# Two-layer decoder: expert results scattered to token order, row sends spread over fewer steps, three bias copies placed behind the last expert block

## The chip, the cores and the metric

The kernel runs on one core of one Trainium2 chip. A core has a matrix engine (TensorE, PE in the profile; its weight loads are listed as PEld), three engines for elementwise work (VectorE or DVE, ScalarE or ACT, GpSimd or POOL), a sync engine that only issues transfers (SyncE or SP), and 16 DMA engines that carry all transfers. Each engine runs its own instructions in order; semaphores tie the engines together. The metric is the device time of one execution in microseconds, lower is better.

## The reference, cut to what matters

The program is a pre-norm decoder of two layers over 32 sequences of 100 tokens (3200 tokens of 256 numbers, float32). Each layer has self-attention, cross-attention over 361 context rows, and a mixture of experts. The change touches the end of Layer 0 and the start of Layer 1:

```python
# Layer 0's experts: 8 experts of width 704, the best 2 per token, plus a shared one of width 352
logits = x @ gate_w
top_v, top_i = jax.lax.top_k(logits, 2)
top_p = jax.nn.softmax(top_v, axis=-1)
combine = zeros((T, 8)).at[arange(T)[:, None], top_i].add(top_p)
d = einsum('tei,eih->teh', silu(x @ Wg) * (x @ Wu), Wd)
out = einsum('te,teh->th', combine, d) + silu(x @ Sg) * (x @ Su) @ Sd

# Layer 1's self-attention: causal, no softmax
k, q, v = split(x @ W1 + b1, 3)
attn = where(mask, q @ k^T, 0.0)
out = (attn @ v) @ W2 + b2
```

## The kernel before

The token array x stays in SBUF as 25 tiles of 128 tokens (NF = 25). PE's order is written out by hand; on the other engines the instructions stand in an order that a scheduler finds when the program is built. Waits between engines are derived from the data, and `depend` adds further ones by hand.

**Up to the experts (0 to about 1100 us).** Layer 0's self- and cross-attention. While it runs, SP fills work arrays in device memory (`stage_weights`, L1100 on): all expert weights in one array `w_d`, zeros in `xe_d` (L1115, the rows sorted by expert) and zeros in those parts of `y_d` (L1118, the experts' results in the same order) that belong to blocks that seldom run. Normalized token rows are written into a tile that takes the place of a weight tile, `self.rows` (L455), 256 numbers per row, tile after tile.

**Shared expert and row sends (about 1100 to 1182 us).** PE works through the shared expert in groups of four tiles: `hidden(f)` makes the products w of gate and up (ACT L1197, DVE L1198), and `down(f)` of a group two steps back multiplies by the third matrix and adds into x (DVE L1207). Beside this GpSimd sends each token's row to its two places in `xe_d`: `scatter` (L1158 to L1168) is one indirect DMA of 128 rows (issued at L1160), 50 in all, tile after tile with both choices k = 0 and k = 1 of a tile one after the other. `tick` spreads them: each DVE result of the shared expert is a tick, and after tick t of N_TICKS = 34 (L1209) the same fraction of the 50 sends may have gone. A send waits for the DVE result at whose tick it was placed.

**Expert blocks (1182 to about 1592 us).** 29 blocks run always: 24 of 256 rows and 5 of 128 rows (the fourth, the tenth and so on are such half blocks). For each, `load0` (L1272) lets GpSimd gather the weights of the block's expert (2.2 MB, L1277, three buffers) and SP load the block's rows (L1285, three buffers) two blocks ahead; the load waits for all 50 sends. `turn0` (L1294) transposes the rows on PE while the block before is computed. `block0` (L1326) is six chunks: PE makes gate and up, ACT the activation g, DVE the product h (L1341; for the last chunk of 64 columns a copy u, L1349, and two products, L1354 and L1356), then PE multiplies by the third matrix (L1362, and L1368 for the last chunk), ACT and DVE copy the results to y (L1373, L1374), and SP writes y to `y_d` (L1375). `behind` (L1238) places small work behind chosen blocks, tied to the block's last DVE copy (`self.late`): loads of Layer 1's weights (L1248), and behind the fifth block copies of the slot table and the probabilities (L1241), which Layer 1 needs.

After the 29 blocks every engine reads a count (L1251) and skips the remaining blocks (`tc.If`, L1252) if all rows have been dealt with, as they have in these runs.

**Layer 1's self-attention (about 1595 to 1815 us).** First PE makes values for the following cross-attention (L703, L155 into `v`, ACT L149). `gather0` (L1255) then brings the two expert results of every token: two indirect DMAs per tile on GpSimd by the slot table (issued at L1261, eight buffers), and DVE adds each, times its probability, to x (L1266). Norms follow (DVE L196 to L208, square root on ACT L202), and then the attention itself, sequence by sequence: `proj` (q and k; ACT L973 and L970), `scores` (PE, then DVE L1002 with the mask), `vals` (DVE L983), `values` (PE L1012, ACT L1019), `out` (DVE L260). The gathers and norms of a group of four sequences are spread over the work on an earlier group. Three small DVE operations in `l1_attn` prepare the biases of q and k (L942 twice, L943); the scheduler is free to place them as early as it sees fit.

Layer 1's cross-attention and experts fill the rest.

Of the kernel before, what the change touches and what calls it, by code (L numbers as in the profile page):

```python
# [9 lines left out]
F32 = mybir.dt.float32  # L10
I32 = mybir.dt.int32
# [32 lines left out]

XROW = D + 1 + E1

HALVES = {0: 6, 6: 6, 12: 6, 18: 7}
# [51 lines left out]
class Kernel:  # L99
# [331 lines left out]
    def l0_xattn(self):  # L431
        nc, tc, a = self.nc, self.tc, self.a
        with ExitStack() as st:
# [14 lines left out]
            for h in range(H):  # L448
# [5 lines left out]

            self.rows = self.wts.tile([P, 8192], F32, tag="wA", name="wAn")[:, : NF * D].rearrange(  # L455
                "p (f d) -> p f d", f=NF
            )

# [23 lines left out]
            for t in ks:  # L482
                nc.gpsimd.memset(t[:, :, :, L:], 0.0)
            later = deque()
            ctx, q, q2, e, es = {}, {}, {}, {}, {}
# [435 lines left out]
    def l1_attn(self):  # L921
        nc, tc, a = self.nc, self.tc, self.a
        with ExitStack() as st:
# [17 lines left out]
            for j in range(2):  # L941
                nc.vector.tensor_scalar(bias[:, j, :], bqk[:, 0, :], own[:, j : j + 1], None, ALU.mult)  # L942
            nc.vector.tensor_copy(bias[:, 2, :], bqk[:, 2, :])  # L943
            vs = [cp.tile([T, H, 32], F32, tag=f"v{i}", name=f"v{i}") for i in range(3)]
# [155 lines left out]
    def stage_weights(self):  # L1100


        nc, a = self.nc, self.a
        dram = self.ctx.enter_context(
            self.tc.tile_pool(name="dram0", bufs=1, space=bass.MemoryType.DRAM)
        )
        self.w_d = dram.tile([E0 * P, WROW], F32, tag="w_d", name="w_d")
        self.xe_d = dram.tile([ROWS0, D], F32, tag="xe_d", name="xe_d")
        self.y_d = dram.tile([ROWS0, D], F32, tag="y_d", name="y_d")
        with self.tc.tile_pool(name="zero", bufs=1) as zp:  # L1110
            zero = zp.tile([P, 2048], F32, tag="zero", name="zero")
            nc.gpsimd.memset(zero, 0.0)
            xe = self.xe_d.rearrange("(i p r) d -> i p (r d)", p=P, r=8)
            for i in range(ROWS0 // (8 * P)):
                nc.sync.dma_start(xe[i], zero)  # L1115
            for j in REST0:
                y = self.y_d[rows0(j)[0], :].rearrange("(p r) d -> p (r d)", p=P)
                nc.sync.dma_start(y, zero[:, : y.shape[1]])  # L1118
        for e in range(E0):
            row = self.w_d[e * P : (e + 1) * P, :]  # L1120
            for k in range(NK):
                for j, n in enumerate(("wg0", "wu0")):
                    src = a[n][e][k * P : (k + 1) * P, :]
                    o = k * 2 * I0
                    nc.sync.dma_start(row[:, o + 640 * j : o + 640 * (j + 1)], src[:, :640])
                    nc.sync.dma_start(
                        row[:, o + 1280 + 64 * j : o + 1280 + 64 * (j + 1)], src[:, 640:]
                    )
            o = 2 * NK * I0
            src = a["wd0"][e]  # L1130
            for c in range(5):
                nc.sync.dma_start(row[:, o + c * D : o + (c + 1) * D], src[c * P : (c + 1) * P, :])

            for j in range(2):
                nc.sync.dma_start(row[64 * j : 64 * j + 64, o + 5 * D :], src[640:, :])

    def l0_ffn(self):
# [3 lines left out]
        with ExitStack() as st:  # L1141
# [16 lines left out]
            def scatter(after):  # L1158
                f, k = divmod(len(sent), 2)
                got = nc.gpsimd.indirect_dma_start(  # L1160
                    out=self.xe_d[:, :],
                    out_offset=bass.IndirectOffsetOnAxis(ap=slot[:, f, k : k + 1], axis=0),
                    in_=xn[:, f, :], in_offset=None,
                    bounds_check=ROWS0 - 1, oob_is_err=True,
                )
                tc.declare_no_dep(got.ins, group="xe", reason="other rows")
                tc.add_to_no_dep_group("xe", got.ins)
                self.depend(got, [after.ins], "not faster than the work beside it")  # L1168
                sent.append(got.ins)
# [38 lines left out]

            N_TICKS = NF + 3 * 6 - 9  # L1209
            with tc.manual_schedule(engines={mybir.EngineType.PE}):  # L1210
# [21 lines left out]
            o = 6144 + 1536  # L1232
            slot1 = self.wa1.bitcast(I32)[:, o : o + 2 * NF].rearrange("p (f k) -> p f k", k=2)
            pr21 = self.wa1[:, o + 2 * NF : o + 4 * NF].rearrange("p (k f) -> p k f", k=2)
            self.picked0 = slot1, pr21

            def behind(j):
                if BLOCKS0 - 5 < j < BLOCKS0 - 1:  # L1238
                    self.depend(self.load1(j - BLOCKS0 + 4), [self.late.ins], "behind the block")
                if j == 4:  # L1240
                    for got in (nc.vector.tensor_copy(slot1, slot), nc.vector.tensor_copy(pr21, pr2)):  # L1241
                        self.depend(got, [self.late.ins], "behind the block")

                room = 4 if j > 1 else 0
                while room > 0 and self.loads:
# [3 lines left out]
                    self.depend(got, [self.late.ins], "behind the block")  # L1249
            self.blocks0_run(pool, ORDER0, wid, hs, sent, behind)  # L1250
            n = nc.values_load(self.blocks0[0:1, 0:1], min_val=0, max_val=NBLK)  # L1251
            with tc.If(n > 0):  # L1252
                self.blocks0_run(pool, REST0, wid, hs, [], lambda i: None)

    def gather0(self, pool, f, after=None):  # L1255

        nc = self.nc
        slot, pr2 = self.picked0
        for k in range(2):
            y = pool.tile([P, D], F32, tag="yk", name="yk", bufs=8)  # L1260
            nc.gpsimd.indirect_dma_start(  # L1261
                out=y, out_offset=None, in_=self.y_d[:, :],
                in_offset=bass.IndirectOffsetOnAxis(ap=slot[:, f, k : k + 1], axis=0),
                bounds_check=ROWS0 - 1, oob_is_err=True,
            )
            got = nc.vector.scalar_tensor_tensor(  # L1266
# [6 lines left out]
    def load0(self, pool, j, wid, sent):  # L1273
# [7 lines left out]
        )  # L1281
        xe = pool.tile([P, 2, D], F32, tag="xe", name="xe", bufs=3)
        at, n = rows0(j)
# [10 lines left out]
    def turn0(self, pool, xe):  # L1294
# [8 lines left out]
        self.evac(xT, pt)  # L1303
        return xT

    def blocks0_run(self, pool, js, wid, hs, sent, behind):

        with self.tc.manual_schedule(engines={mybir.EngineType.PE}):
            ready = [self.load0(pool, j, wid, sent) for j in js[:2]]
            w, xe = ready.pop(0)  # L1310
            xT = self.turn0(pool, xe)
            for i, j in enumerate(js):
                got = []
                if i + 2 < len(js):
                    ready.append(self.load0(pool, js[i + 2], wid, sent))

                def turn():
                    if ready:
                        w, xe = ready.pop(0)
                        got.extend((w, self.turn0(pool, xe)))  # L1320

                self.late = self.block0(pool, j, w, xT, hs[i % 2], turn)
                behind(i)
                if got:
                    w, xT = got

    def block0(self, pool, j, w, xT, h, turn):
# [46 lines left out]
        done = nc.vector.tensor_copy(y[:, 0, :], py[0])  # L1374
        nc.sync.dma_start(self.y_d[at, :].rearrange("(s p) d -> p s d", p=P), y)  # L1375
        return done

# [708 lines left out]
```

## Time and profile before

| | us |
|---|---|
| median of 3 runs (lowest to highest) | 2970.16 (2968.84 to 2970.37) |
| profiled execution | 2999.12 |
| its span, first to last instruction | 2997.4 |
| mean granted TensorE clock in it | 0.981 |

The parts of the kernel that the change is about, in the profiled execution:

| what | measured |
|---|---|
| expert block of 256 rows, from weight gather to weight gather | 15.08 to 15.12 us in undisturbed stretches |
| half block | 8.30 us |
| GpSimd row send or gather of 128 rows, one | 0.98 to 1.04 us busy |
| zero fill of `y_d` | 7 transfers, issued between 30.96 and 45.9 us |
| expert results to `y_d` | 29 SP writes, 24 of 256 KB and 5 of 128 KB |
| results back in Layer 1 | 50 GpSimd gathers, 1595.9 to 1720 us |

How to read the lines further down. A line of a timeline has the start (us from the span's start), the length, the engine, the line of the kernel, the operation, output and input tiles, shapes, and how many instructions it stands for; in brackets the engine's idle time just before and what ended it ("issue": nothing that the profile shows). Names of tiles are those of the program: `xe` a block's rows, `w` weights or a product in the same tile, `ps_t` a PSUM bank, `y` a block's result, `yk` a gathered result, `wAn` the normalized rows, `kT` and `qT` keys and queries. A line of windows has the stretch, its length, then busy time and instruction count of PE, PEld, DVE, ACT and POOL, then PE's granted clock as a fraction of full speed, the DMA engines' mean busy share, and GB/s.

### The profile page before, as it was taken

Reading aid. Unit: us, or ns where it says so; the run is one execution under the profiler, and the core shown is the slowest. Engines: PE = TensorE matmul, PEld = TensorE weight load, DVE = VectorE, ACT = ScalarE, POOL = GpSimd, SP = SyncE. Lnnn points to the kernel's source line nnn. Section 1 sums busy time; section 2 is a strip of 40 time slices with the busy share of each in tenths; the row PEclk is TensorE's granted clock in tenths of the full one; section 3 lists DMA queues with packets and bytes.
Section 4 is the critical chain, followed back from the end, with each engine's and each line's share of the span. In section 5 each row is a group of like instructions: output and inputs, shape, how many; then the busy total and the mean of one; then the engine's idle time right before and its main releaser. Section 6 shows DMA issues by size and latency. Waiting matters only on the chain. (4 is left out here: it accounts for less than half of the span.)

```text
span 2997.4 us, 66479 instructions
## 1 busy us (share of the span) xinstructions
PE 2866.1 (96%) x26012; PEld 2176.5 (73%) x26012; DVE 1789.8 (60%) x5120; ACT 1415.9 (47%) x4261; POOL 914.0 (30%) x1040
## 2 busy tenths in 40 slices
PE   8999999999999999999998999999999999998993
PEld 7777777677777756888885667777777777775672
DVE  6665666577777742222225778676666676776454
ACT  5554555567666631221223224565566566566220
POOL 3222221266655544100005431021311212123364
PEclk9999999999999989999998999999999999999997
DMA  9870000000000023654552100010000000000297
GB/s 316 272 276 1 1 1 1 14 15 16 15 15 15 8 87 122 211 202 183 199 217 74 32 2 10 6 42 20 26 11 12 12 12 11 12 10 5 83 229 194
DMA packets 127511, 224.12 MB, mean 75 GB/s; under 512 B 39470, under 2 KB 105446, under 8 KB 120401
## 3 DMA queue, kind: packets, MB, share of 16 engines
q1 hardware_dynamic: 97264, 125.64, 13.2%
q0 software_dynamic: 26640, 90.80, 9.3%
q8 instruction: 210, 3.44, 0.5%
q10 hardware_dynamic: 3280, 3.28, 0.3%
q14 instruction: 117, 0.95, 0.1%
HBM read 152.09 MB, written 112.56 MB: 88 GB/s over the span
## 5 line engine op out<-in xcount | busy, mean ns | idle before, releaser
L1682 POOL DMA_INDIRECT x_d<-xr,slot x200 | 195.5, 977 | 663.6 <-ACT eT L785 571.5
L155 PE MATMUL ps_t<-xnT,wA 128*128 128x200 f32 (+1 forms) x1608 | 329.9, 349 | 1.5 <-DMA wA<-in_wq 0.9
L155 PE MATMUL ps_t<-cT,q 128*128 128x361 f32 x832 | 317.4, 470 | 1.4 <-ACT wBx L775 1.4
L785 ACT COPY eT<-ps_t 124x384 f32<-124x384 f32 (+1 forms) x416 | 194.4, 476 | 229.7 <-PE ps_t L784 227.2
L775 ACT ACTIVATE wBx<-ps_t,m 128x361 f32<-128x361 f32 x416 | 236.7, 570 | 126.4 <-DVE m L772 118.6
L155 PEld LDWEIGHTS ps_t<-xnT,wA 128*128 128x128 f32 x1608 | 271.1, 191 | 32.4 <-issue 12.9
L534 DVE TENSOR_REDUCE m<-ps_t 100x1 f32<-100x361 f32 x512 | 239.6, 525 | 46.3 <-PE ps_t L155 46.1
L155 PE MATMUL ps_t<-xT,w 128*128 128x256 f32 (+1 forms) x1276 | 262.4, 365 | 0.7 <-ACT xT L149 0.7
L772 DVE TENSOR_REDUCE m<-ps_t 128x1 f32<-128x361 f32 x416 | 218.6, 527 | 60.8 <-PE ps_t L155 57.1
L155 PEld LDWEIGHTS ps_t<-xT,w 128*128 128x128 f32 x1276 | 225.1, 191 | 37.2 <-issue 9.6
L784 PEld LDWEIGHTS ps_t<-ident,wBx 128*124 128x124 f32 x1248 | 156.3, 140 | 123.1 <-issue 69.8
L357 POOL TENSOR_TENSOR e<-e,rz 100x400 f32<-100x400 f32 x128 | 109.5, 856 | 406.7 <-DVE rz L356 396.8
L556 ACT ACTIVATE e<-ps_t 121x300 f32<-121x300 f32 x512 | 173.9, 426 | 118.4 <-PE ps_t L155 118.3
L784 PE MATMUL ps_t<-ident,wBx 128*124 128x128 f32 x1248 | 204.7, 275 | 3.2 <-DVE sums L776 1.2
L353 ACT ACTIVATE e<-s,m 100x100 f32<-100x100 f32 x512 | 186.6, 368 | 21.2 <-DVE m L347 20.6
L155 PE MATMUL ps_t<-wA,cT 128*124 128x512 f32 x384 | 196.5, 600 | 0.0
L777 DVE TENSOR_SCALAR wBx<-wBx,sums 128x361 f32<-128x361 f32 x416 | 173.1, 416 | 9.9
L1341 DVE TENSOR_TENSOR h<-ps_t,g 128x256 f32<-128x256 f32 (+1 forms) x145 | 58.1, 402 | 186.1 <-ACT g L1340 186.1
L155 PEld LDWEIGHTS ps_t<-q,k 32*121 32x121 f32 x3072 | 128.0, 181 | 35.9 <-issue 11.3
L796 PEld LDWEIGHTS ps_t<-eT,v 124*64 124x64 f32 x3072 | 134.6, 137 | 23.1 <-issue 12.1
L796 PE MATMUL ps_t<-eT,v 124*64 124x100 f32 x3072 | 143.1, 250 | 4.9 <-issue 4.8
L1277 POOL DMA_INDIRECT w<-w_d,wid x29 | 29.6, 1019 | 376.0 <-PE ps_t L1368 343.7
(329 smaller groups left out, 5749.0 us busy)
## 6 DMA issues: line engine op xcount, KB each, us to landing
x_d<-fill SPq DMA_DIRECT2D x16, 1284.0 KB
we<-in_wexp SPq DMA_DIRECT2D x32, 384.0 KB
cT<-in_ctxT SPq DMA_DIRECT2D x64, 186.0 KB
xe_d<-zero SPq DMA_DIRECT2D x8, 1024.0 KB
xe<-x_d SPq DMA_DIRECT2D x24, 321.0 KB
sum<-fill SPq DMA_DIRECT2D x10, 640.0 KB
xe<-xe_d SPq DMA_DIRECT2D x24, 256.0 KB
y_d<-y SPq DMA_DIRECT2D x24, 256.0 KB
```

Of the source, the lines that this page charges most:

```text
L155: self.nc.tensor.matmul(out, lhsT=l, rhs=r, start=(i == 0), stop=(i == n - 1))
L353: nc.scalar.activation(t[:, i, :], s[:, i, :], AF.Exp, bias=m[:, i : i + 1], accum_out=rz[:, i : i + 1])
L357: nc.gpsimd.tensor_tensor(t[:, h, :], t[:, h, :], self.last(rz[:, h], T), ALU.mult)
L534: got = nc.vector.tensor_reduce(m[:, j, o : o + 1], ps[r], AX.X, ALU.max, negate=True)
L556: nc.scalar.activation(t[:, r], ps[r].rearrange("p (c t) -> p c t", c=NKC), AF.Exp)
L772: self.after = nc.vector.tensor_reduce(m, ps, AX.X, ALU.max, negate=True)
L775: nc.scalar.activation(t, ps, AF.Exp, bias=m, accum_out=z)
L777: nc.vector.tensor_scalar(t, t, z, None, ALU.mult)
L784: nc.tensor.transpose(pt[:, c, :], es[n % 5][:, c * KC : (c + 1) * KC], self.ident)
L785: self.after = nc.scalar.copy(eT[:, :, i * P : i * P + w], pt[:, :, :w])
L796: nc.tensor.matmul(pz[64 * j : 64 * j + 64, i, :], lhsT=v[:, c, h * 64 : (h + 1) * 64], rhs=eT[:, c, o : o + T], start=(c == 0), stop=(c = ...
L1682: got = nc.gpsimd.indirect_dma_start(out=self.x1_d[:, :], out_offset=bass.IndirectOffsetOnAxis(ap=slot[:, j, k : k + 1], axis=0), in_=xr[: ...
```

## The change

1. A normalized row gets a 257th word, its token's number: GpSimd makes the numbers once and copies them in. `xe_d`, the tile `xe` and the rows use a pitch of 257 words; unused rows of `xe_d` carry the number 2 x 3200, which lies outside the result array and makes a write drop.
2. The sends run through all tiles for k = 0 first and then for k = 1. Before the sends of k = 1, GpSimd adds 3200 to the numbers, five tiles at a time, so that the second result of a token gets a row of its own. N_TICKS falls from 34 to 29.
3. `y_d` has 6400 rows in token order (first results, then second ones) and isn't filled with zeros.
4. Per block, DVE copies the rows' numbers from float to integer (`ids`, three buffers), and GpSimd scatters the results to `y_d` by them, one indirect DMA per 128 rows (53 in the 29 blocks), issued after the next weight gather. SP's writes go.
5. In Layer 1, 25 SP loads (both results of a tile, 256 KB, six buffers) replace the 50 gathers. They wait for a GpSimd operation that follows the last scatter (`y_done`). In the skipped branch a second flag and a one-word load let SP wait for the additional blocks' scatters.
6. The slot table isn't copied any more. The three bias operations of Layer 1 wait for the last block's last DVE copy (`self.late`).

```diff
-            self.rows = self.wts.tile([P, 8192], F32, tag="wA", name="wAn")[:, : NF * D].rearrange(
-                "p (f d) -> p f d", f=NF
-            )
+            rows = self.wts.tile([P, 8192], F32, tag="wA", name="wAn")[:, : NF * ROW0]
+            self.rows0 = rows = rows.rearrange("p (f d) -> p f d", d=ROW0)
+            self.rows = rows[:, :, :D]
...
+            ids = cp.tile([P, NF], F32, tag="ids", name="ids")
+            nc.gpsimd.iota(ids, pattern=[[P, NF]], base=0, channel_multiplier=1,
+                           allow_small_or_imprecise_dtypes=True)
+            nc.gpsimd.tensor_copy(rows[:, :, D], ids)
...
             for j in range(2):
-                nc.vector.tensor_scalar(bias[:, j, :], bqk[:, 0, :], own[:, j : j + 1], None, ALU.mult)
-            nc.vector.tensor_copy(bias[:, 2, :], bqk[:, 2, :])
+                got = nc.vector.tensor_scalar(bias[:, j, :], bqk[:, 0, :], own[:, j : j + 1], None, ALU.mult)
+                self.depend(got, [self.late.ins], "behind the last block")
+            got = nc.vector.tensor_copy(bias[:, 2, :], bqk[:, 2, :])
+            self.depend(got, [self.late.ins], "behind the last block")
...
-            for j in REST0:
-                y = self.y_d[rows0(j)[0], :].rearrange("(p r) d -> p (r d)", p=P)
-                nc.sync.dma_start(y, zero[:, : y.shape[1]])
...
             def scatter(after):
-                f, k = divmod(len(sent), 2)
+                k, f = divmod(len(sent), NF)
+                if k and f % 5 == 0:
+                    id1 = self.rows0[:, f : f + 5, D]
+                    nc.gpsimd.tensor_scalar_add(id1, id1, float(NT))
                 got = nc.gpsimd.indirect_dma_start(
                     out=self.xe_d[:, :],
                     out_offset=bass.IndirectOffsetOnAxis(ap=slot[:, f, k : k + 1], axis=0),
-                    in_=xn[:, f, :], in_offset=None,
+                    in_=self.rows0[:, f, :], in_offset=None,
...
-            N_TICKS = NF + 3 * 6 - 9
+            N_TICKS = NF + 3 * 6 - 14
...
-            self.blocks0_run(pool, ORDER0, wid, hs, sent, behind)
+            put = self.blocks0_run(pool, ORDER0, wid, hs, sent, behind, "y0")
+            self.y_done = nc.gpsimd.memset(self.y_flag[:, 0:1], 0.0)
+            self.depend(self.y_done, put, "the blocks' results")
...
+        y2 = pool.tile([P, 2, D], F32, tag="yk", name="yk", bufs=6)
+        got = nc.sync.dma_start(y2, self.y_d.rearrange("(k f p) d -> f p k d", k=2, p=P)[f])
+        self.depend(got, [self.y_done.ins], "the blocks' results")
         for k in range(2):
-            y = pool.tile([P, D], F32, tag="yk", name="yk", bufs=8)
-            nc.gpsimd.indirect_dma_start(
-                out=y, out_offset=None, in_=self.y_d[:, :],
-                in_offset=bass.IndirectOffsetOnAxis(ap=slot[:, f, k : k + 1], axis=0),
-                bounds_check=ROWS0 - 1, oob_is_err=True,
-            )
+            y = y2[:, k, :]
...
         self.evac(xT, pt)
-        return xT
+        ids = pool.tile([P, 2], I32, tag="ids", name="ids", bufs=3)[:, :n]
+        self.nc.vector.tensor_copy(ids, xe[:, :, D])
+        return xT, ids
...
+        def send(y, ids):
+            for s in range(y.shape[1]):
+                got = nc.gpsimd.indirect_dma_start(
+                    out=self.y_d[:, :],
+                    out_offset=bass.IndirectOffsetOnAxis(ap=ids[:, s : s + 1], axis=0),
+                    in_=y[:, s, :], in_offset=None,
+                    bounds_check=2 * NT - 1, oob_is_err=False,
+                )
+                tc.declare_no_dep(got.ins, group=group, reason="other rows")
+                tc.add_to_no_dep_group(group, got.ins)
+                put.append(got.ins)
...
                 if i + 2 < len(js):
                     ready.append(self.load0(pool, js[i + 2], wid, sent))
+                if result:
+                    send(*result)
...
         done = nc.vector.tensor_copy(y[:, 0, :], py[0])
-        nc.sync.dma_start(self.y_d[at, :].rearrange("(s p) d -> p s d", p=P), y)
-        return done
+        return done, y
```

The copies `ids` in the changed kernel stand at its line 1317, the scatters of results at L1326, the loads of both results at L1273.

## The prediction

> **What bounds the kernel now.** I read the page's busy table first, then the lengths of the Layer 0 expert blocks (each starts with GpSimd's weight gather, L1277), then the timelines of VectorE (DVE), TensorE (PE) and GpSimd (POOL) where something the diff touches sits beside a PE gap.
>
> ```profile
> PE 2866.1 (96%) x26012; PEld 2176.5 (73%) x26012; DVE 1789.8 (60%) x5120; ACT 1415.9 (47%) x4261; POOL 914.0 (30%) x1040
> ```
>
> PE is the bound: an edit counts only if it opens or closes a PE gap or moves PE's clock. I found four places.
>
> ```profile
> 1404.91 0.36 DVE L942 TENSOR_SCALAR bias<-wB,own 128x2 f32<-128x2 f32 x2 [5.12 <-DMA xe<-xe_d]
> 1405.52 1.22 PE L1362 MATMUL ps_t<-w,h 128*128 128x256 f32 x2 [2.86 <-DVE h L1341]
> ...
> 1380.83:1395.70 14.87, 14.87 (x73) 12.58 (x72) 3.79 (x11) 2.84 (x9) 1.01 (x2) 1.00 0.50 186
> 1395.70:1408.16 12.46, 9.60 (x60) 7.74 (x60) 2.67 (x11) 2.26 (x8) 1.00 (x1) 0.89 0.59 221
> 1408.16:1425.44 17.28, 17.28 (x74) 14.31 (x74) 4.07 (x11) 2.71 (x8) 1.01 (x2) 0.88 0.44 154
> ```
>
> First place: DVE sits 5.12 us at Layer 1's bias (L942), whose weights have not landed; h, queued behind it, is late and PE stands 2.86 us. In the rows of windows (bounds, length, busy PE, PEld, DVE, ACT, POOL, granted clock, DMA share, GB/s) the block with the stall lasts 12.46, the next 17.28, at clocks 0.89 and 0.88.
>
> ```profile
> 1112.43 0.98 POOL L1160 DMA_INDIRECT xe_d<-wAn,slot  x1 [1.21 <-DMA w<-w_d,wid]
> 1166.54 0.69 DVE L1198 TENSOR_TENSOR w<-ps_t,w 96x512 f32<-96x512 f32 x1 [2.74 <-issue]
> 1171.46 2.97 PE L155 MATMUL ps_t<-xnT,wBs 128*128 128x128 f32 x24
> 1175.58 0.98 POOL L1160 DMA_INDIRECT xe_d<-wAn,slot  x1 [1.83 <-DVE x_sb L1207]
> 1178.25 4.68 SPq L1285 DMA_DIRECT2D xe<-xe_d  x4
> 1181.96 0.60 PE L1299 MATMUL ps_t<-ident,xe 128*128 128x128 f32 x4
> ```
>
> Second place: the last row send is at 1175.58, SyncE (SP) loads the first blocks' rows at 1178.25, PE takes them at 1181.96 without idling.
>
> ```profile
> 1222.76 0.42 DVE L1341 TENSOR_TENSOR h<-ps_t,g 128x256 f32<-128x256 f32 x1 [1.30 <-ACT g L1340]
> 1223.21 0.29 DVE L1349 COPY u<-ps_t 64x128 f32<-64x128 f32 x1
> 1227.63 0.70 PE L1368 MATMUL ps_t<-w,h 64*128 64x256 f32 x4
> ```
>
> Third place, inside every block: between the fifth h and u DVE is free at 1223.18; PE needs the last h at 1227.63.
>
> ```profile
> 1639.32:1667.58 28.26, 26.76 (x310) 17.13 (x310) 19.39 (x56) 5.67 (x16) 13.94 (x14) 0.82 0.14 41
> 1667.58:1695.48 27.90, 24.86 (x299) 16.29 (x301) 19.87 (x54) 5.76 (x16) 11.64 (x12) 0.94 0.17 46
> 1695.48:1721.45 25.97, 24.39 (x326) 16.87 (x328) 21.35 (x53) 6.70 (x17) 18.17 (x19) 0.93 0.09 25
> 1721.45:1743.30 21.85, 21.67 (x314) 14.61 (x308) 18.66 (x51) 5.78 (x17) 2.41 (x3) 1.00 0.01 2
> ...
> 1646.64 0.44 PE L155 MATMUL ps_t<-qT,kT 32*100 32x100 f32 x5 [0.30 <-issue]
> 1647.36 0.32 PE L155 MATMUL ps_t<-qT,kT 32*100 32x100 f32 x1 [0.29 <-issue]
> ...
> 2788.41 0.42 PE L796 MATMUL ps_t<-eT,v 124*64 124x100 f32 x5 [0.26 <-issue]
> 2789.15 0.42 PE L796 MATMUL ps_t<-eT,v 124*64 124x100 f32 x5 [0.32 <-issue]
> ```
>
> Fourth place: Layer 1's attention, cut at its kT rows, one group of four sequences a window. While POOL gathers expert results (until 1720) a group takes 28.26, 27.90, 25.97; afterwards 21.85. PE's gaps there are "issue", a few matmuls per 0.72 us. The only other such comb, 2787 to 2791, lies beside a run of POOL row sends (1.29 us apart). Beside large matmuls (sends 1102 to 1175) there is none.
>
> **The change part by part.**
>
> *Bias behind the last block.* Gone: 12.46 against the half block's usual 8.30 (gathers at 1312.17 and 1320.47), and 17.28 against 15.12 (the whole block from 1320.47): 4.16 + 2.16 = **-6.3**. Bounds: -4.2 (if the slow clock comes back elsewhere) to -6.3. The three small DVE operations now run behind the branch, where DVE idles 6.6 us before its first L1266.
>
> *The id copy (f32 to int32, 128x2), 29 times.* DVE converts such shapes in 0.17 to 0.18 (its small CASTs); DVE is busy 3 to 4 us of a 15 us block. What it waits for matters, and DVE takes instructions in order. In the changed kernel's compiled order the first three copies stand inside the shared expert: two ahead of the product w at 1166.54, the third right behind it, ahead of the x update of 1167.77. They wait for the rows' loads, which wait for the last send. Behind them are all the shared expert's remaining products; PE's first matmul that waits for that w stands at 1172.80, the seventh of the twelve inside the row at 1171.46.
>
> When does the last send go? There are 50 of them, at a period of 1.29 from 1102.41. The eighth still waits for the first weight gather (1112.43). Fourteen are out at 1120.2; two id additions (0.3 each, by POOL's 0.21 COPY of 128x3) and the second weight gather follow at 1122.3; the 22nd waits for its landing (11.5 after issue, as for the first): 1134. The 25th goes at 1138.4, and the additions for the last rows wait for its landing: 2.67 later, the distance from the last send to SP's load above. The 25 of k=1 then run from 1141.4 at 1.29: the last at 1172.4. DVE's steps that pace them all come earlier (the last at 1160.4). So the denser schedule buys 3 us. Loads at 1175.1; before, the first landed 2.7 after issue (SP's wait for it ended at 1180.96), the third at about 4 (last packet 1182.00): 1177.8 to 1179. DVE then makes w by 1179.2, and PE stands from 1172.80 to 1179.2. It then runs without the 0.93 gap it has at 1175.36: 6.4 - 0.9 = 5.5 late. For the clock, between the 2.16 lost after the 2.86 gap and a little more, 2.5: **+8.0**. Bounds: 0 (sends at 1.29 throughout, no landing waits: last at 1167) to +11.2 (last send at 1175.58 as now).
>
> The clock gate by the Trainium skill, "TensorE: Matmul & The Clock Gate", section "What's actually happening": after an idle window of about 3.4 us PE runs at half clock until about 3.4 us of activity; this would make the 2.5 an estimated 1.7, and would charge the bias stall's 2.86 us nothing, where the rows show 2.16.
>
> *In the blocks.* POOL sends a block's results (two indirect DMAs at 1.3) behind the next weight gather. They share its queue: the first sends after the gather of 1100.87 move no packet until 1109.27. In the blocks the gather's packets end 8.4 to 10.6 after the block's start B; results land perhaps 1 later, B+9.4 to B+11.6. With three buffers, the id copy of a later block waits for them, between the fifth h (B+9.4) and u. Last h may be 1227.63 - 1224.51 = 3.1 late; less the copy, the wait may end at B+12.3. After the half blocks one copy stands ahead of the fifth h, with B+10.5 as limit; one of those four gathers ends at 10.64. I take **+0.5**, bounds 0 and +17 (results at B+13.0 in 24 whole blocks: 0.7 each). POOL works 1 us of 15 there, so 2.6 more is covered. SP's 29 y writes go; nothing waits for SP's issue.
>
> *Gathers become 25 SP loads of 256 KB.* The 50 POOL gathers (1.01 each) leave Layer 1. The first eight are hidden: rstd's square root stands behind ACT's last v copy (1611.54), though DVE has its sums at 1609.26. The combs are the question. If the gathers cause them, three groups come down to 21.85: 6.4 + 6.1 + 4.1 = 16.6, less one gap of 1.5 (at 1716.24) that waits for DVE's s; PE's 3.23 gap at 1619.20 and the slow clock behind it might add 5. Bounds: 0 to -20. I take **-12**: the match in two places is strong, but the profiled execution is 29 us longer than the runs, and such issue gaps may be partly its own.
>
> Against it stands the Trainium skill, "DMA: Bandwidth & Descriptors", section "Issuing engines are not separate DMA queues": transfers of all engines run on the same 16 DMA engines and interleave, so moving them saves only issue time. By that rule alone this term is 0 and the total +2.2.
>
> *The rest.* At the branch PE's own 3.5 us compare stands (gap 3.54 at 1595.28). The last scatter goes at about 1592.5, lands at 1595.2, the flag and the first loads follow at 1595.6, data at 1598.3, against 1598.84 now; if that were 2.3 late PE would wait. Seven zero-fills (1.4 MB at the start), slot copy and pitch 257 cost or give nothing: PE's first work hides the fills, and norm rows into a 321-word pitch take 0.42, into 256 words 0.65.
>
> **Sum:** -6.3 + 8.0 + 0.5 - 12 = -9.8 on the profiled 2999.1 (span 2997.4), so 2989.3; the runs' median, 29.0 lower, becomes **2960.4**.
>
> **The rivals.** (A) The combs stay, with SP's loads or without: -6.3 + 8.0 + 0.5 = +2.2, **2972.4**. For it: matching in time is not cause. Against: the group without gathers has the same work and no gap. (B) Combs and the slow start of Layer 1 go entirely, or sends are early: -6.3 + 5 + 0 - 20 = -21, **2949**. (C) Slower: results land late behind the weight gather and hold DVE at the id copy in every whole block. Point: past B+12.3 each microsecond costs 24; at B+13.0, 17 more than my forecast, **2977**; it decides from B+12.9. For it: SP writes them now in a queue of their own. Against: the gathers' packets end by B+10.6. (D) Id copies don't wait on the chip as ordered, term 0: **2952**.
>
> **How the numbers follow.** A measurement can tell about 0.2% (5.9 us) from no change. Forecast 0.47 (2955 to 2968), A 0.22, B and D 0.14, C and a later load together 0.17. Faster: most of the forecast, B and D, a little of A: 0.57. Same: the forecast's slow end and most of A: 0.22. Slower: C and the upper end of A: 0.21. Range 2946 to 2978, with a tenth outside at either end.
>
> **What would show it.** Bias: blocks at 8.30 and 15.1 around 1400. Id copies: DVE idle some 14 us before L1317 near 1165, PE some 6 before L155, slow clock after. In blocks: L1317 waits under 3 us, lengths unchanged. Combs: no "issue" gaps between 1637 and 1696, groups near 22. The forecast is wrong if PE has no gap near 1173, if groups stay at 26 to 28, or if blocks lengthen.

## The result and the profile after

The changed kernel takes 2979.02 us (median of 8 runs, 2974.22 to 2981.89), the kernel before beside it 2970.77 (8 runs, 2968.84 to 2976.96). The ratio is 1.0023 with a 95% interval of [1.0013, 1.0034]: about 8 us slower, where the forecast was 9.8 faster; the interval lies above 1, though the difference is small (0.2%). The profiled execution of the changed kernel took 2974.22, the fastest of the eight, its span 2972.5; that of the kernel before had taken 2999.12. So the two profiles say "25 us faster" and the runs say "8 us slower". Most of what follows is about this contradiction.

The page's busy table, first row:

```profile
PE 2850.7 (96%) x26012; PEld 2170.1 (73%) x26012; DVE 1789.4 (60%) x5148; ACT 1414.9 (48%) x4261; POOL 916.8 (31%) x1052
```

PE has the same 26012 matmuls and is 15.4 us less busy than in the profile of before. Now the places that the prediction named. First the timelines of VectorE and TensorE at the end of the shared expert (start, length, engine, line, operation, idle time before it and what ended that):

```profile
1177.85 0.17 DVE L1317 CAST ids<-xe 128x2 int32<-128x2 f32 x1 [15.11 <-DMA xe<-xe_d]
1178.59 0.17 DVE L1317 CAST ids<-xe 128x2 int32<-128x2 f32 x1 [0.57 <-DMA xe<-xe_d]
1178.67 0.69 DVE L1206 TENSOR_TENSOR w<-ps_t,w 96x512 f32<-96x512 f32 x1
1179.77 0.17 DVE L1317 CAST ids<-xe 128x2 int32<-128x2 f32 x1 [0.42 <-DMA xe<-xe_d]
...
1179.41 2.94 PE L156 MATMUL ps_t<-xnT,wBs 128*128 128x128 f32 x12 [7.50 <-DVE w L1206]
```

DVE stands 15.11 us at the first id copy, because the rows it reads have not landed. The product w, whose last input ACT had made by 1164.28, is queued behind two such copies, and PE stands 7.50 us for that w.

Next the windows of the blocks around the former bias stall and of the first four groups of Layer 1's attention (bounds, length, busy PE, PEld, DVE, ACT, POOL, granted clock, DMA share, GB/s):

```profile
1402.65:1410.95 8.30, 8.30 (x61) 7.40 (x61) 2.42 (x9) 2.27 (x8) 3.02 (x4) 1.00 0.79 281
1410.95:1426.07 15.12, 15.12 (x74) 12.80 (x73) 4.20 (x13) 2.70 (x8) 2.05 (x3) 1.00 0.56 202
1635.70:1661.50 25.80, 24.65 (x339) 16.69 (x338) 23.51 (x63) 5.78 (x17) 4.61 (x6) 0.93 0.19 53
1661.50:1683.60 22.10, 21.94 (x307) 14.96 (x308) 18.81 (x52) 5.56 (x17) 2.50 (x3) 1.00 0.13 38
1683.60:1706.12 22.52, 22.42 (x314) 15.81 (x318) 19.80 (x55) 6.56 (x18) 14.26 (x15) 1.00 0.05 13
1706.12:1727.94 21.82, 21.64 (x314) 14.59 (x308) 18.63 (x51) 5.77 (x16) 2.42 (x3) 1.00 0.01 2
```

The bias stall is gone: the half block takes 8.30 (12.46 before), the next 15.12 (17.28), at clock 1.00. The second and third group of Layer 1 take 22.10 and 22.52 and have no issue gaps; the first keeps 25.80: its window holds 339 matmuls, the others 307 to 314, and PE waits 0.94 us in it for DVE's s.

The view of the tile ids, and GpSimd's timeline at the end of the blocks:

```profile
its engine sat idle before it (us, times) until:
  DMA y_d<-y,ids: 42.9, 26
...
DMA to landing us min/median/max: 3.5/8.5/9.9
```

```profile
1593.34 0.97 POOL L1326 DMA_INDIRECT y_d<-y,ids  x1 [5.65 <-DVE y L1408]
1597.34 0.09 POOL L1257 MEMSET yflag<- 1x1 f32 x1 [3.03 <-DMA y_d<-y,ids]
```

The lines "its engine sat idle" mean that DVE, before 26 of the id copies, waits 42.9 us in all for results to land; a landing comes 8.5 us (median) after its issue, most behind a weight gather. At most 3.29 us go to one copy, PE has no gap over 0.2 us in the blocks from the second one on, and whole blocks keep their 15.08: these waits lie under PE's work. The last scatter lands 4.0 us after its issue.

### The profile page after: what moved, and what is told of

It reads as the page before. It is cut to its first block, busy times and chain, and to the rows that moved or that the text cites. A ratio compares the mean times of both kernels' runs of the same rounds, so it can differ in the third digit from the quotient of the medians.

```text
span 2972.5 us, 66506 instructions
## 1 busy us (share of the span) xinstructions
PE 2850.7 (96%) x26012; PEld 2170.1 (73%) x26012; DVE 1789.4 (60%) x5148; ACT 1414.9 (48%) x4261; POOL 916.8 (31%) x1052
## 3 DMA queue, kind: packets, MB, share of 16 engines
q10 hardware_dynamic: 3280, 3.28, 0.3%
## 5 line engine op out<-in xcount | busy, mean ns | idle before, releaser
L1374 ACT ACTIVATE g<-ps_t 128x256 f32<-128x256 f32 (+1 forms) x145 | 53.0, 366 | 190.8 <-PE ps_t L156 190.8
L781 DVE RECIPROCAL sums<-sums 128x1 f32<-128x1 f32 x416 | 66.2, 159 | 124.2 <-ACT wBx L780 123.1
```

## Experiments

All runs are beside runs of the kernel before on the same chip, in six sets; "a set of 2974" is one in which the kernel before takes about 2974 us. An issue gap is idle time of PE for which the profile shows no wait. The first set, three kernels.

**e1_before_again**: the kernel before, unchanged.

> The kernel before, unchanged, profiled and timed again. Theory (the combs belong to single executions, not to the gathers as such): its profiled execution has no or few issue gaps between 1637 and 1696 us, its span lies within 10 us of its timed runs (2969 to 2977), and the changed kernel's gain of 16 us there was none. Rival (gathers cause the combs in every execution, and the profiled one is no exception): the span is again 20 us or more above the timed runs, with groups of 26 to 28 us. The ratio of its times to the kernel before is 1.000 within 0.001.

Measured: 2973.97 (all runs of before in this set 2974.48), ratio 1.0000 [0.9991, 1.0009]; profiled 2973.95. Windows of the same four groups of Layer 1:

```profile
1632.01:1657.29 25.28, 23.97 (x339) 16.30 (x338) 23.06 (x63) 5.67 (x17) 18.72 (x19) 1.00 0.24 67
1657.29:1679.80 22.51, 22.20 (x307) 15.17 (x308) 18.87 (x52) 5.55 (x16) 10.59 (x11) 1.00 0.18 49
1679.80:1702.96 23.16, 23.00 (x314) 15.88 (x317) 20.45 (x55) 6.57 (x19) 19.18 (x20) 1.00 0.10 27
1702.96:1724.80 21.84, 21.66 (x314) 14.60 (x308) 18.66 (x51) 5.77 (x16) 2.74 (x4) 1.00 0.04 11
```

GpSimd is busy with the gathers (18.72, 10.59 and 19.18 us), and the groups take 25.28, 22.51 and 23.16, not 28.26, 27.90 and 25.97. The gathers alone do not make the issue gaps. The first group takes some 25 us even without them.

**e2_bias_only**: of the change, only the bias part, in the kernel before.

```diff
-                nc.vector.tensor_scalar(bias[:, j, :], bqk[:, 0, :], own[:, j : j + 1], None, ALU.mult)
+                got = nc.vector.tensor_scalar(bias[:, j, :], bqk[:, 0, :], own[:, j : j + 1], None, ALU.mult)
+                self.depend(got, [self.late.ins], "behind the last block")
...
```

> The kernel before with only the three bias operations placed behind the last block. Theory: the half block of 12.5 us and the block of 17.3 us return to 8.3 and 15.1, 6.3 us less: 2964.5, ratio 0.9979. Rival (the stall was of one execution only, as the combs): ratio 1.000.

Measured: 2966.63, ratio 0.9972 [0.9963, 0.9981]; in its profile the half block is back at 8.30 and the next at 15.12.

**e3_ids_behind_turn**: the changed kernel, each id copy tied behind the copy of its turned rows, so that it stands behind all of the shared expert's products on DVE.

```diff
-        self.evac(xT, pt)
+        turned = self.evac(xT, pt)
...
-        self.nc.vector.tensor_copy(ids, xe[:, :, D])
+        got = self.nc.vector.tensor_copy(ids, xe[:, :, D])
+        self.depend(got, [turned.ins], "behind the turned rows")
```

> The changed kernel with each id copy made to wait for the same block's transposed rows, so that the first three leave the middle of the shared expert. Theory: PE's 7.5 us gap near 1179 goes, first block some 7 us earlier, 1 to 3 us of slow clock with it: 2971 to 2972 against 2979 for the changed kernel, ratio to the kernel before 1.000 to 1.001. Rival (the changed kernel's loss sits elsewhere, in Layer 1 or in the blocks): the gap goes but the time falls by less than 3 us.

Measured: 2967.14, ratio 0.9976 [0.9967, 0.9985]. PE has no gap at 1173 any more; the 24 matmuls that had stood apart by 7.50 us run through:

```profile
1174.18 2.82 PE L156 MATMUL ps_t<-xnT,wBs 128*128 128x128 f32 x24
```

With the stall cured, the changed kernel is worth just what the bias part is worth alone; the loads in place of gathers add nothing here. Taken together with e1, the picture was: copies +8, bias -7, gathers 0, and a profile of before that was one odd execution. The second set did not bear that out.

**e4_after_again**: the changed kernel, unchanged.

> The changed kernel as it is, on the same chip as the three below. Theory 1 (the id copies ahead of w cost about 8 us at 1173, the bias gives 6 to 8 back, Layer 1's start costs 1 to 2, the gathers give nothing): ratio to before 1.000 to 1.001, and 8 us above e3_ids_behind_turn's 0.9976. Theory 2 (the changed kernel holds a further loss of some 5 us that its first profile, the fastest of its runs, did not show): ratio 1.002 or more again, and a place in the second trace that is later than in the first beyond the 8 us at 1173.

Measured: 2992.32, and the kernel before 2999.60: ratio 0.9975 [0.9966, 0.9984]. Both theories missed. In this set the kernel before takes what its first profile had shown, and the changed kernel is 7.3 us faster.

**e7_before_third**: the kernel before, for its profile.

> The kernel before once more, for its profile. Theory 1 (the issue gaps of PE beside the gathers, and the 27 us by which the profiled execution stood above the runs, belong to that one execution): time within 2969 to 2983, groups of Layer 1's first attention near 22 us, no issue gaps of 0.3 us between 1637 and 1696. Theory 2 (they come and go with the gathers): gaps there again, with a time near 2985 to 3000.

Measured: 3003.59. Windows of the four groups:

```profile
1639.80:1665.88 26.08, 24.87 (x318) 16.69 (x315) 22.59 (x61) 5.78 (x16) 13.64 (x14) 0.87 0.16 44
1665.88:1692.05 26.17, 23.29 (x299) 15.56 (x301) 20.01 (x54) 5.76 (x17) 11.65 (x12) 1.00 0.18 50
1692.05:1718.28 26.23, 24.54 (x296) 16.70 (x294) 21.55 (x56) 6.67 (x18) 18.21 (x19) 0.91 0.08 24
1718.28:1741.69 23.41, 23.34 (x334) 15.65 (x337) 18.00 (x49) 5.89 (x15) 2.42 (x3) 0.95 0.01 2
```

The slow groups beside the gathers are back, in a set in which all 21 runs of before lie between 2994.91 and 3005.47. So the long time belongs neither to one execution nor to the profiler, but to the whole set.

**e5_scatter_alone**: e3_ids_behind_turn with the biases prepared where they were before (e2's diff undone).

> The kernel of e3_ids_behind_turn with the biases prepared where they were before: so only the scatter to tokens' order, the denser sends and the loads of results remain, with the id copies behind the turned rows. Theory 1 (exchanging 50 gathers for 25 loads gives nothing, the bias is worth 6 to 8 us): ratio to before 0.999 to 1.001, no PE issue gaps beside Layer 1's first groups here or in before. Theory 2 (the loads do give the 12 us of the prediction, and something else in the changed kernel takes them back): ratio 0.997 or less.

Measured: 2998.49, ratio 0.9997 [0.9988, 1.0006]. The ratio is the one expected, the reasons are not: the groups of Layer 1 do gain some 12 us here, and the shared expert takes them back. TensorE's timeline there:

```profile
1167.08 3.19 PE L156 MATMUL ps_t<-wBs,w 128*128 128x256 f32 x14
1170.79 0.46 PE L156 MATMUL ps_t<-wBs,w 128*128 128x256 f32 x1 [0.53 <-issue]
1172.87 0.38 PE L156 MATMUL ps_t<-wBs,w 128*128 128x256 f32 x1 [1.62 <-issue]
1176.37 0.58 PE L156 MATMUL ps_t<-wBs,w 96*128 96x256 f32 x1 [3.12 <-issue]
1177.77 3.91 PE L156 MATMUL ps_t<-wBs,w 96*128 96x256 f32 x7 [0.81 <-issue]
```

No id copy is in the way, and still PE issues single matmuls 1.4 to 3.5 us apart. It waits for nothing that the profile shows. Beside it GpSimd has been sending rows every 1.29 us without a break since about 1144, 21 of them before the first gap. In e3, whose kernel differs from this one by the bias part alone, 25 sends follow each other at the same pace without any such gap; e3 ran in the set of 2974.

**e6_sends_34**: the changed kernel with its sends spread over 34 steps, as before the change. The built order then also has the id copies behind the last w.

```diff
-            N_TICKS = NF + 3 * 6 - 14
+            N_TICKS = NF + 3 * 6 - 9
```

> The changed kernel with the row sends spread over 34 steps as before instead of 29. The built order then puts the first three id copies behind the last w product and among the last x updates. Theory 1 (the 8 us come from the copies' place ahead of w on VectorE): PE's gap at 1173 shrinks to under 2 us although the last send goes about 3 us later, and the time is 4 to 8 us below that of e4_after_again. Theory 2 (the 8 us come from the late landing of the first blocks' rows, wherever the copies stand): the gap grows by the 3 us that the denser sends had bought, the time is 3 above e4_after_again.

Measured: 2986.17, ratio 0.9957 [0.9943, 0.9970], 6.2 below e4. The stall near 1173 is gone; PE waits 1.82 us for the first rows at 1182. This edit changes the pace of the sends and the place of the copies at once, so it does not say which of the two cured the stall.

The third set was for the pace of the sends: **e8_after_third** (the changed kernel), **e9_sends34_again** (as e6), **e10_sends34_ids_behind_turn** (e6 and e3 together) and **e11_before_sends29** (the kernel before with N_TICKS lowered by 5 and nothing else).

> The changed kernel once more. The kernel before has taken 2974 on one chip and 3000 on another, with PE issue gaps beside the gathers only on the second. Theory 1 (the chips differ in these gaps, and so does what the change is worth): if before takes about 2974 here, the ratio is 1.000 to 1.003 and the groups beside the former gathers are alike in both; if it takes about 3000, the ratio is 0.997 to 0.9985. Theory 2 (the ratio is the same on all chips and the earlier two differ by chance): 0.999 to 1.001 either way.

> The changed kernel with its sends over 34 steps, as before. Theory 1 (it takes away the stall near 1173 on both kinds of chip, by id copies that stand behind w and by breaks between the sends): 0.9955 to 0.9965 where before takes about 3000, 0.997 to 0.999 where it takes about 2974, 8 to 12 us below e8_after_third. Theory 2 (its gain on the chip of 3000 was that chip's issue gaps alone): no different from e8_after_third where before takes about 2974.

> Sends over 34 steps and the id copies behind the turned rows: the version meant to beat both kernels. Theory 1 (two causes of one stall, each cured by its own edit): PE without a gap between 1165 and 1182 on any chip, 2 to 4 us below e9_sends34_again, since the 1.8 us that PE waits there for the first rows at 1182 shrink or stay. Theory 2 (one cure is enough): equal to e9_sends34_again within 2 us.

> The kernel before with its 50 sends over 29 steps and nothing else changed: no ids, no scatter, gathers as before. Theory 1 (on the slower kind of chip some twenty sends back to back hold up the other engines' issue): where before takes about 3000, PE gets issue gaps between 1160 and 1180 if this order leaves 20 or more sends 1.29 apart, and 2 to 9 us are lost; where it takes about 2974, the time is that of before within 2 us. Theory 2 (the stall needs the id copies or the rows' landing): no change on either.

Measured, with before at 3006.13: e8 2995.77, ratio 0.9964 [0.9952, 0.9976]; e9 2988.60, 0.9941 [0.9929, 0.9953], 7.2 below e8 (8 to 12 expected); e10 2989.69, 0.9940 [0.9926, 0.9954]; e11 3010.11, 1.0012 [1.0002, 1.0021]. In e10 PE still waits 3.28 us for the first rows at 1186.01, so the expected "no gap" missed, and one cure is enough in this set. e11 shows what the pace does by itself, a little earlier than expected:

```profile
1151.00 2.11 PE L155 MATMUL ps_t<-wBs,w 128*128 128x256 f32 x9
1154.40 0.59 PE L155 MATMUL ps_t<-wBs,w 128*128 128x256 f32 x2 [1.29 <-issue]
1155.82 0.38 PE L155 MATMUL ps_t<-wBs,w 96*128 96x256 f32 x1 [0.83 <-issue]
1157.22 5.48 PE L155 MATMUL ps_t<-wBs,w 128*128 128x256 f32 x12 [1.03 <-issue]
```

GpSimd's next send stands in its timeline so:

```profile
1158.31 0.99 POOL L1160 DMA_INDIRECT xe_d<-wAn,slot  x1 [3.71 <-DVE w L1198]
```

There are three issue gaps, at the end of a run of sixteen sends 1.29 us apart; then the sends pause 3.71 us and the gaps stop, though PE runs its next twelve matmuls at half its pace (5.48 us, against 5.36 for 24 elsewhere). There are no ids and no scatter in this kernel.

The last three sets asked whether the result comes back with the kind of set: **e12_after_fourth**, **e13_sends34_third** (as e6) and **e14_bias_only_again**; **e15_sends34_ids_behind_turn** (as e10) and **e16_bias_only_third**; **e17_sends34_ids_behind_turn** and **e18_after_fifth**.

> The changed kernel once more. Theory 1 (what the change is worth goes with the issue gaps beside GpSimd's indirect transfers): ratio 1.000 to 1.003 in a set where before takes about 2974 and shows no issue gaps, 0.996 to 0.998 in a set where it takes about 3000. Theory 2 (the first measurement of 1.0023 was an accident): 0.996 to 0.9985 in a set of 2974 too.

> The changed kernel with its sends over 34 steps. Theory 1: 0.997 to 0.999 in a set of 2974 (no stall near 1173, because the id copies stand behind w there), 0.994 to 0.996 in a set of 3000. Theory 2 (its gain is made only of issue gaps): as e12_after_fourth in a set of 2974.

> The kernel before with its biases prepared behind the last block, which measured 0.9972 in a set of 2974. Theory 1 (the bias is worth 6 to 8 us everywhere, the loads of results 12 to 14 more only where the issue gaps are): 0.997 to 0.998 in any set, above e13_sends34_third by 8 us or more in a set of 3000, within 3 us of it in a set of 2974. Theory 2 (the bias gain too is larger or smaller with the issue gaps): outside 0.9965 to 0.9985 in a set of 3000.

> Sends over 34 steps and id copies behind the turned rows, the candidate for the best kernel on both kinds of set. Theory 1 (bias minus 6 to 7, Layer 1's start plus 2, the stall cured, gathers only where issue gaps are): 0.9975 to 0.999 in a set of 2974, 0.993 to 0.995 in a set of 3000. Theory 2 (sends over 34 steps bring a loss of their own, as 0.9993 for sends alone against 0.9976 for the moved copies alone may say): 0.999 or more in a set of 2974.

> The kernel before with only its biases behind the last block. Theory 1 (one mechanism, independent of issue gaps): 0.997 to 0.998 in any set; in a set of 3000 above e15 by 10 us or more, in a set of 2974 at or below e15. Theory 2 (its gain goes with the issue gaps): outside 0.9965 to 0.9985 in a set of 3000.

> The candidate once more, for a set in which before takes about 2974. Theory 1: 0.9975 to 0.999 there, 0.993 to 0.995 in a set of 3000. Theory 2 (sends over 34 steps bring a loss of their own): 0.999 or more in a set of 2974.

> The changed kernel in the same set as the candidate. Theory 1: 1.002 to 1.0035 in a set of 2974, 0.996 to 0.998 in a set of 3000, 8 to 13 us above the candidate in either.

Ratios of four kernels to the kernel before, by the time of before in their set:

| kernel | before about 2972 | before about 3003 |
|---|---|---|
| changed kernel | 1.0023 [1.0013, 1.0034]; e12 1.0032 [1.0019, 1.0044]; e18 1.0025 [1.0016, 1.0034] | e4 0.9975 [0.9966, 0.9984]; e8 0.9964 [0.9952, 0.9976] |
| bias part alone | e2 0.9972 [0.9963, 0.9981]; e14 0.9978 [0.9969, 0.9987] | e16 0.9976 [0.9965, 0.9986] |
| changed, sends over 34 steps | e13 0.9993 [0.9984, 1.0002] | e6 0.9957 [0.9943, 0.9970]; e9 0.9941 [0.9929, 0.9953] |
| that and ids behind the turn | e17 0.9976 [0.9967, 0.9986] | e10 0.9940 [0.9926, 0.9954]; e15 0.9941 [0.9927, 0.9955] |

The last row beats both kernels in either kind of set: 2966.70 against 2982.68 of the changed kernel in e17's set, 2989.69 against 2995.77 in e10's. Also outside what was expected lie e8 (below 0.997), e9 (below 0.9955), e12 (above 1.003), e16 (9.1 us over e15 instead of 10 or more) and e18 (16.0 over e17 instead of 8 to 13). e13 came out above its expectation, 4.6 us over e14; some 2 of them lie in the stage of Layer 1's last sends (165.5 against 163.7), and their cause was not found.

PE's order is the same in all kernels, so the time between the same two matmuls can be compared. Stage lengths from one profile each (us, from PE's starts; in the profile of the prediction the stages begin at 1061.0, 1182.0, 1600.0, 1717.0 and 2732.8, and the last one ends at 2901.6):

| | shared expert | Layer 0's blocks | Layer 1's first attention | on to Layer 1's last sends | those sends |
|---|---|---|---|---|---|
| before, e1 (set of 2974) | 119.2 | 419.3 | 99.1 | 1010.4 | 163.7 |
| changed, first profile | 129.1 | 413.6 | 99.6 | 1010.3 | 163.3 |
| changed, e18 (set of 2973) | 131.1 | 412.0 | 99.5 | 1010.4 | 167.7 |
| last row above, e17 | 119.9 | 412.9 | 99.5 | 1010.0 | 163.4 |
| before, profile of the prediction | 121.0 | 418.1 | 116.9 | 1015.8 | 168.8 |
| before, e7 (set of 3000) | 119.8 | 419.8 | 111.2 | 1018.0 | 172.1 |
| before with dense sends, e11 | 126.4 | 417.3 | 117.1 | 1016.6 | 170.0 |
| changed, e8 (set of 3006) | 132.3 | 412.0 | 100.6 | 1016.2 | 173.4 |
| last row above, e15 | 122.3 | 416.3 | 99.7 | 1016.1 | 172.2 |

The kernel before needs 12 to 18 us more for Layer 1's first attention in the sets near 3003, and 10 to 16 more in the next two stages, where GpSimd sends Layer 1's rows. The change takes away the first, and touches nothing of the rest.

## Why the prediction was wrong

The step that failed is the gather term, "I take **-12**", with the one that carried it over to the runs: "so 2989.3; the runs' median, 29.0 lower, becomes **2960.4**". The sum was made on a profile whose execution stood 29 us above the runs, and those 29 us were taken as an offset that lies evenly around the change. They were not. Some 18 of them lay in the very stage that the -12 was to be won from (116.9 against 99.1 in e1). PE stood about 6 us in issue gaps beside the gathers (those over 0.2 us between 1636 and 1722), and its granted clock was 0.82 to 0.94 in the three groups where e1 shows 1.00. The runs had no such loss, as far as e1's profile of a run of 2973.95 shows, so nothing was to be won. The prediction wrote that such gaps "may be partly its own", and yet gave the case that they stay 0.22 and the forecast 0.47. It also counted the first group's 6.4 us among what could come down; that group takes 25.28 in e1 and 25.80 after the change, without issue gaps.

Term by term:

- **Bias, -6.3.** Right. Layer 0's blocks lose 6 to 7 us in the kernels with this part, and alone it gives 0.9972, 0.9978 and 0.9976, with medians 5.8 to 8.3 us lower. Only the kernels with sends over 34 steps in the sets near 3003 lose less there (e15: 416.3): PE waits for the first rows, and its first block is then 2.7 to 3.0 us longer.
- **Id copies in the shared expert, +8.0.** Right in place and mechanism, but too small for the runs: the forecast had the last send at 1172.4, DVE's copies from 1177.8 and PE standing from 1172.80 to 1179.2; measured were 1172.49, 1177.85, and PE standing from 1171.9 to 1179.41. Against its own profile (121.0) the first profile after shows +8.1. But that profile already held a gap of 0.93 us in this stage and slow clock behind it, some 1.8 us in all over e1. Against e1's 119.2 the three profiles after take 9.9, 11.4 (e12) and 11.9 (e18) more, two of them beyond the bound of 11.2. e3, where only the copies' place differs, and e17, where the sends' pace differs too, have the stage back at 119.2 and 119.9.
- **The clock in that term, 2.5.** The 42 matmuls from the end of the gap to the first block take 7.82 us in e1, and 1.6 more in the first profile (granted clock 0.57 from 1179.41 to 1183.00), 2.6 in e12 and 3.0 in e18 (0.50 to 0.52 until 1187). So 2.5 was a fair size. Its basis was misread: the 2.86 us gap of the bias had cost not 2.16 but 3.46 us of clock, since PE was busy 9.60 us in the block of the stall where 8.30 are usual. By the Trainium skill, "TensorE: Matmul & The Clock Gate", section "What's actually happening", an idle window of about 3.4 us is followed by half clock until there have been about 3.4 us of activity, which makes an estimated 1.7 us of loss. That fits the first profile and not the other two.
- **Id copies inside the blocks, +0.5.** Right: results land late enough to hold DVE 42.9 us in all, and the cover named for it (DVE free until PE needs the last h) holds. Rival C fell: whole blocks keep 15.08.
- **Gathers to loads, -12.** Nothing won in the sets near 2972: the stage takes 98.5 to 99.1 with gathers (e1, e2, e14) and 99.4 to 100.7 with loads. In the sets near 3003 it becomes 11 to 18 us shorter. There the sum holds: 2989.3 to 2999.1 is a ratio of 0.9967, and 0.9975 and 0.9964 were measured. But it is partly luck that it does, since the loss in the shared expert has another cause there than the +8.0 names (see the row sends). The rule of the Trainium skill that was set against the term, "DMA: Bandwidth & Descriptors", section "Issuing engines are not separate DMA queues", under which the term is 0, agrees with the sets near 2972 and not with those near 3003.
- **Row sends, 3 us sooner for nothing.** Missed: the prediction saw that beside large matmuls sends made no issue gaps, but only for the old pace. In the sets near 3003 the first gap comes at the end of 16 (e11) or 21 (e5) sends 1.29 us apart, and the stage takes 126.4 (e11; 119.8 in e7) and 129.9 (e5). e5 has no id copy ahead of w and still loses as much there as the changed kernel (129.4 in e4). In the sets near 2972 the same pace costs nothing (e3: 119.2).
- **The branch, put at nothing.** The last scatter lands 4.0 us after its issue (2.67 assumed), and the first results are added at 1600.61. PE falls up to 3.6 us behind at 1636 (e17 against e14, counted from the first block) and is still 1.3 behind at 1691.

The signs that were to show the forecast right came in the main: a gap near 1173, the second and third group near 22, blocks unchanged. The first group stayed at 25.80, and a few waits of L1317 reached 3.29 us instead of 3. These signs could not tell, because the second and third group of before are near 22 too in the sets that count (22.51 and 23.16 in e1). Rival A, "the combs stay", had the right consequence for the wrong reason: there were none to stay. Its 2972.4 lacks the larger stall.

The terms measured in the sets near 2972 (copies +10 to +12, bias -6 to -7, gathers 0) give +3 to +6; the runs show +7 to +9.5. Part of the rest lies in Layer 1's first attention, where the loads are not quite free (e12 takes 100.7 there, e14 in the same set 98.5). The remainder lies in stages that the change leaves alone (up to the shared expert, Layer 1's last sends), which differ by up to 4.4 us between profiles of one kernel. It stays open.

## What to carry to other kernels

Before a stall read from a profile is put into a sum, compare the profiled execution with the runs: where it stands apart by more than the effect looked for, find out in which stages the surplus lies, and don't count as gain what the runs may not have. An instruction that waits for a transfer must not be put ahead of ready work on an engine that runs in order: tying it behind that work here was one more dependency, and no cost of it was seen (e3). A denser stream of transfers need not be free just because its engine is idle: here it cost nothing in one kind of set and some 6 to 10 us in the other.

## What was not expected of the hardware

The same kernel takes about 2972 in some sets of runs and about 3003 in others, all runs of a set alike, at nearly the same mean clock (in the profiles of before 0.984 and 0.979 to 0.981). The chip does not tell the two apart, as far as its number names it: chips 1 and 6 each had one set of either kind. What differs is PE, issuing single matmuls or a few at a time in steps near multiples of 0.7 us beside long rows of GpSimd's indirect transfers, in three places (gathers of Layer 0's results, dense row sends, Layer 1's row sends), though the transfers are issued at the same 1.3 us in both kinds. The two queues that the profile calls "instruction" move the same number of packets in both (210, and 115 to 117). What holds PE up is not shown by any record here.

The scatters of results, nearly all issued behind a 2.2 MB gather on GpSimd's queue, landed 8.5 us after their issue in the median of all 53, the last one, which had no gather ahead, after 4.0.
